# The order of a group's last step in a frequency mix: the two last pairs of S and the last spreading ahead of the fourth turn

## The chip, the cores and the metric

The kernel runs on one core of one Trainium2 chip. The metric is the device time of one execution in microseconds (us). Lower is better.

## What is computed

The input is x of 16 batches x 16 channels x 256 x 256 in float32. Two layers follow each other, each adding something to its group-normalised input. Only the first one matters here:

```python
alpha = fft2(gn(x))                                      # b i o x: batch, channel, row and column frequency
A  = 1 / (omega1 - weights_pole1)                        # o i k p
Bm = 1 / (omega2 - weights_pole2)                        # x i k q
S  = einsum('ikpq,oikp,xikq->oxik', weights_residue, A, Bm)
output_residue1 = einsum('biox,oxik->bkox', alpha, S)    # the mix: 16x16 matrix for every frequency (o, x)
x1 = ifft2(output_residue1).real
...                                                      # x2, a second term from the poles
x  = x + x1 + x2 / Nx / Ny
```

The second layer (two convolutions, an involution, a gate) uses most of the remaining time and is not touched.

## The kernel before, in words

The program has four parts, one after the other: `layer0_forward` (normalisation, forward transforms, tables), `layer0_mix`, `layer0_back` (inverse transform along the rows, the pole term, and the sum), and `layer1`. The change lies in `layer0_mix`.

The mix works on 33 groups of row frequencies (g = 0 to 32). A group has four row frequencies, f = 0 to 3; the last group has only one that counts. In a group these things are done:

- `poles` (L625 to L635): VectorE makes `lt`, the row factors of S, with six products (L629).
- `residues` (L639 to L653): TensorE multiplies `lt` with the table `tt` (matmuls of L643) into a PSUM buffer `ps`, for one channel k at a time; a call makes two channels. VectorE copies the odd channels into the tile `s` (L651), ScalarE the even ones (L653). Eight calls fill S for all 16 channels.
- `spread` (L617 to L620): the loaded spectrum `alc` is multiplied with a mask and written into `alb`, the right operand of the mix. There are 16 such `expand`s for a group: six on ScalarE (L605), ten on VectorE (L607). They are dealt out over the steps by a table; for f = 3 only one is left, on VectorE.
- `mix` (L655 to L672): for each of 64 x 4 column frequencies one matmul of `s` with `alb` (L665) into PSUM buffers `pg`, eight buffers' worth in sequence. ScalarE copies each into `y` (L672).
- `turn` (L674 to L688): for one f, eight TensorE transposes of `y` (L681) into two PSUM buffers `pt`. VectorE copies the first into `yt` (L687), ScalarE the second (L685).
- `columns` (L690 to L723): for one f, TensorE's inverse transform along the columns (L700) into `ph`. ScalarE copies the odd part (L709), VectorE adds and subtracts (L712, L713), and the result `h` leaves for `hd` by DMAs from POOL's queue (L720).

The groups are pipelined by hand. `s` and `lt` have one buffer, and so has `y`. S and `alb` of the next group are made during the four steps of this group, and the columns of f = 3 are put off into the mix of the next group, as a generator `between`, of which one part is taken at each of x0 = 24 and x0 = 48. `ps` of S and `pg` of the mix share four PSUM buffers, and `pt` has two.

The order of the instructions on TensorE, ScalarE, VectorE and POOL is the order in which the program calls them (`manual_schedule`); each engine works on its own list in order and waits at semaphores for the others. So the loop at L747 sets the order:

```python
for f in range(4 if more else 1):
    yt = turn(y, f)
    if more:
        if f == 3:
            spread(spectrum, f)
        for k0 in range(2 if f == 0 else 4 * f, 4 * f + 4, 2):
            residues(lt, s, k0)
        if f < 3:
            spread(spectrum, f)
        ...
    between = columns(g, f, yt)
```

In this order the step f = 3 has, on TensorE, 8 transposes and then 32 matmul records of S; on VectorE the `yt` copy, one `expand`, and the copies of channels 13 and 15; on ScalarE the `yt` copy and the copies of channels 12 and 14. After that the next group's `poles` and `mix` follow.

Of the kernel before, what the change touches and what calls it, by code (L numbers as in the profile page):

```python
# [553 lines left out]
def layer0_mix(ctx, tc, d, al, hd, tabs):  # L554
# [10 lines left out]
    def load_poles(g):  # L565
        av = ap.tile([P, 32, 4, 3], F32, tag="av", name="av")
        nc.sync.dma_start(out=av.rearrange("p k f l -> p (k f l)"), in_=avd[g])
        return av
# [21 lines left out]
    def load_spectrum(g, q):  # L590

        t = gp.tile([P, 4, 2, P], F32, tag="alc", name="alc", bufs=4)
        src = al[g].rearrange("v (j h c) b x -> h (v j) c (b x)", h=2, c=8)
        for h in range(2):
            nc.sync.dma_start(
                out=t[64 * h : 64 * h + 64].rearrange("p b e x -> p (b e x)"),
                in_=src[h, :, :, 4 * q * N : 4 * q * N + 4 * N],
            )
        return t

    def expand(t, q, j, eng):

        dst = alb.rearrange("p (x e) j b -> p b e x j", e=2)[:, 4 * q : 4 * q + 4, :, :, j]
        if eng is nc.scalar:
            eng.activation(dst, t, AF.Copy, scale=m4[:, j : j + 1])  # L605
        else:
            eng.tensor_scalar(dst, t, m4[:, j : j + 1], None, ALU.mult)  # L607
# [9 lines left out]
    def spread(spectrum, f):  # L617
        for eng, parts in zip((nc.scalar, nc.vector), spreads[f]):
            for q, j in parts:
                expand(spectrum[q], q, j, eng)  # L620

    def poles(av):


        lt = lp.tile([P, 2, C, 3, 4, 8], F32, tag="lt", name="lt")  # L625
        shape = [P, C, 4, 8]
        for h in range(2):
            for plane in range(3):
                nc.vector.tensor_tensor(  # L629
                    lt[:, h, :, plane],  # L630
                    av[:, 16 * h : 16 * h + 16, :, plane].unsqueeze(3).to_broadcast(shape),
                    m8.unsqueeze(1).unsqueeze(2).to_broadcast(shape),
                    ALU.mult,
                )
        return lt  # L635

    def residues(lt, s, k0):

        for k in range(k0, k0 + 2):  # L639
            ps = psg.tile([P, 2, N], F32, tag="pg", name="ps")  # L640
            for v in range(2):
                for h in range(2):
                    nc.tensor.matmul(  # L643
                        ps[64 * h : 64 * h + 64, v],
                        lhsT=lt[:, h, k, 1 - v : 3 - v].rearrange("p l f c -> p (l f c)"),
                        rhs=tt[:, h, k],
                        start=True,
                        stop=True,
                    )
            if k % 2:  # L650
                nc.vector.tensor_copy(s[:, :, :, k], ps.rearrange("p v x -> p x v"))  # L651
            else:
                nc.scalar.copy(s[:, :, :, k], ps.rearrange("p v x -> p x v"))  # L653

    def mix(s, y, between):  # L655


        for x0 in range(0, 64, 8):
            if x0 in (24, 48):
                next(between, None)  # L660
            ps = psg.tile([P, 8, 64], F32, tag="pg", name="pg")
            for x in range(8):
                for q in range(4):
                    i = 4 * (x0 + x) + q
                    nc.tensor.matmul(  # L665
                        ps[32 * q : 32 * q + 32, x],
                        lhsT=s[:, i].rearrange("p v k -> p (v k)"),
                        rhs=alb[:, i].rearrange("p j b -> p (j b)"),
                        start=True,
                        stop=True,  # L670
                    )
            nc.scalar.copy(y[:, :, x0 : x0 + 8], ps.rearrange("p x j -> p j x"))  # L672

    def turn(y, f):  # L674

        yt = hp.tile([P, 8, 8, C], F32, tag="yt", name="yt", bufs=2)
        for t0 in range(0, 8, 4):
            pt = pst.tile([P, 4, P], F32, tag="pt", name="pt")
            for t in range(4):
                j = 16 * f + 2 * (t0 + t)  # L680
                nc.tensor.transpose(pt[:, t], y[:, j : j + 2].rearrange("p q x -> p (q x)"), ident)  # L681
            dst = yt[:, :, t0 : t0 + 4].rearrange("p c t k -> p t c k")
            src = pt.rearrange("p t (c k) -> p t c k", k=C)
            if t0:
                nc.scalar.copy(dst, src)  # L685
            else:
                nc.vector.tensor_copy(dst, src)  # L687
        return yt  # L688

    def columns(g, f, yt):  # L690

        ph = [psh.tile([P, 2, N], F32, tag="ph", name="ph") for q in range(2)]
        for e in range(2):
            if e:
                yield
            for n, (c, v) in enumerate(((0, 0), (0, 1), (1, 0), (1, 1))):
                i = 2 * (2 * c + e) + v
                for q in range(2):
                    lanes = slice(64 * q, 64 * q + 64)
                    nc.tensor.matmul(  # L700
                        ph[q][:, e],
                        lhsT=yt[lanes, i].rearrange("p t k -> p (t k)"),
                        rhs=ix[lanes, i],
                        start=n == 0,
                        stop=n == 3,
                    )
        for q in range(2):
            odd = hp.tile([P, 2, P], F32, tag="odd", name="odd", bufs=2)
            nc.scalar.copy(odd, ph[q][:, 1].rearrange("p (v x) -> p v x", v=2))  # L709
            o = hp.tile([P, 2, 2, P], F32, tag="h", name="h", bufs=5)  # L710
            even = ph[q][:, 0].rearrange("p (v x) -> p v x", v=2)
            nc.vector.tensor_tensor(o[:, :, 0], even, odd, ALU.add)  # L712
            nc.vector.tensor_tensor(o[:, :, 1], even, odd, ALU.subtract)  # L713
            o = o.rearrange("p v h x -> p v (h x)")
            fy = 4 * g + f
            for v in range(2):

                if fy % P or v == 0:
                    part = fy // P if fy % P == 0 else v
                    nc.gpsimd.dma_start(  # L720
                        out=hd[fy % 2, part, fy % P // 2, q:nb:2].rearrange("b k x -> b (k x)"),
                        in_=o[:, v],
                    )  # L723

    E = mybir.EngineType
    with tc.manual_schedule(engines={E.PE, E.Activation, E.DVE, E.Pool}):
        spectrum = [load_spectrum(0, q) for q in range(4)]
        lt = poles(av)
        av = load_poles(1)
        s = gp.tile([P, N, 2, C], F32, tag="s", name="s")  # L730
        for k0 in range(0, C, 2):
            residues(lt, s, k0)
        for q in range(4):
            spread(spectrum, q)
        for q in range(4):
            spectrum[q] = load_spectrum(1, q)
        between = iter(())
        for g in range(NF):
            more = g + 1 < NF
            y = gp.tile([P, 64, 64], F32, tag="y", name="y")  # L740
            if more:
                lt = poles(av)
            mix(s, y, between)
            if more:
                s = gp.tile([P, N, 2, C], F32, tag="s", name="s")
                residues(lt, s, 0)
            for f in range(4 if more else 1):  # L747
                yt = turn(y, f)
                if more:
                    if f == 3:  # L750
                        spread(spectrum, f)
                    for k0 in range(2 if f == 0 else 4 * f, 4 * f + 4, 2):
                        residues(lt, s, k0)
                    if f < 3:
                        spread(spectrum, f)
                    if g + 2 < NF:
                        if f == 0:
                            av = load_poles(g + 2)
                        spectrum[f] = load_spectrum(g + 2, f)
                between = columns(g, f, yt)  # L760
                if f < 3:
                    for _ in between:
                        pass
# [774 lines left out]
```

## Time and profile before

| | us |
|---|---|
| three timed runs, median (lowest to highest) | 7067.28 (7063.57 to 7080.53) |
| the profiled execution: its own time | 7081.88 |
| its span | 7080.1 |
| mix: first L665 matmul to last | 1414.4 to 2906.8 |
| one group, from mix to mix | 43.7 to 52.2 |

In the profile PE is TensorE's matmul part, PEld its weight loads, DVE is VectorE, ACT is ScalarE, POOL is GpSimd and SP the queue from which most loads are started. A row of a timeline has the start in us from the beginning of the span, the length, the engine, the line, the operation, the tiles written and read, the number of instructions merged into the row, and in brackets the idle time ahead of it with the engine and line that ended it ("issue" means that the engine waited for nothing that the profile shows). A matmul in float32 leaves two records, so a count of x32 is 16 matmuls. What is done once in a group counts 32 or 33 times in the whole.

### The profile page before, as it was taken

The numbers are of one execution on the slowest core, as the hardware profiler recorded it, in microseconds if no ns is written. First come the engines' busy times: TensorE is split into PE (matmuls) and PEld (weight loads), VectorE is DVE, ScalarE is ACT, GpSimd is POOL, SyncE is SP. The second block draws the span as 40 slices with busy tenths as digits, with TensorE's granted clock in tenths as the row PEclk, the third lists the DMA queues.
The fourth block names the chain that finished last, engine by engine and source line by source line (L and its number), as shares of the span: only waits on it lengthen the run. The fifth ranks groups of instructions, "written<-read, shape, count | busy, mean of one in ns | idle before, by whom it ended". The sixth has DMA issues, their size and how long they took to land. (4 is left out here: it accounts for less than half of the span.)

```text
span 7080.1 us, 144599 instructions
## 1 busy us (share of the span) xinstructions
PE 6544.7 (92%) x55592; PEld 3663.3 (52%) x55592; DVE 5608.9 (79%) x10346; ACT 3835.5 (54%) x5996; POOL 3521.3 (50%) x4614
## 2 busy tenths in 40 slices
PE   7889999899999998899979999999999999999996
PEld 5777778666667666677733333333333333333331
DVE  8999985466667666688878888888888888888885
ACT  2223333365666665322266666666666676666671
POOL 2334445412222222466655666667666667665663
PEclk9899999999999999999989999999999999999998
DMA  3344444433333333699968888889888889888886
GB/s 99 112 115 123 125 120 123 132 95 92 100 99 102 98 96 92 207 326 326 326 191 248 260 257 269 277 278 282 268 257 265 277 281 278 277 258 264 277 272 212
DMA packets 716083, 1443.41 MB, mean 204 GB/s; under 512 B 98954, under 2 KB 525254, under 8 KB 673638
## 3 DMA queue, kind: packets, MB, share of 16 engines
q1 hardware_dynamic: 567206, 959.76, 44.3%
q0 software_dynamic: 148192, 474.40, 21.3%
q8 instruction: 444, 7.27, 0.4%
q14 instruction: 241, 1.97, 0.1%
HBM read 877.12 MB, written 556.47 MB: 202 GB/s over the span
## 5 line engine op out<-in xcount | busy, mean ns | idle before, releaser
L1085 ACT ACTIVATE wide<-c,b 32x512 f32<-32x512 f32 x2176 | 1477.6, 679 | 314.0 <-PE c L1037 265.2
L1116 DVE TENSOR_TENSOR top<-pd,t 32x512 f32<-32x512 f32 x2176 | 1504.0, 691 | 55.8 <-DMA cf<-top 3.2
L1037 PE MATMUL c<-z,w 102*128 102x512 f32 x2048 | 996.4, 618 | 110.5 <-ACT wide L1085 89.0
L1113 DVE TENSOR_TENSOR t<-pd,r 64x512 f32<-64x512 f32 x1088 | 743.8, 684 | 349.0 <-PE pd L1105 322.8
L1097 POOL COPY wide<-wide 32x1031 f32<-32x1031 f32 (+1 forms) x576 | 581.2, 1009 | 882.6 <-ACT wide L1085 855.5
L1105 PE MATMUL pd<-wide,dw 128*128 128x512 f32 x2048 | 994.4, 607 | 13.0 <-DVE top L1116 12.0
L720 POOL DMA_DIRECT2D hd<-h x512 | 323.5, 639 | 1207.1 <-DVE h L713 1182.6
L1037 PEld LDWEIGHTS c<-z,w 102*128 102x128 f32 x2048 | 370.6, 191 | 695.2 <-issue 457.9
L1185 PE MATMUL c2ps<-rows,c 128*32 128x512 f32 x6144 | 721.9, 602 | 5.6 <-DVE odd L1212 5.6
L1105 PEld LDWEIGHTS pd<-wide,dw 128*128 128x128 f32 x2048 | 382.8, 193 | 576.5 <-issue 417.2
L1056 ACT ACTIVATE bot<-c,b 128x512 f32<-128x512 f32 x544 | 343.9, 683 | 462.2 <-issue 383.3
L1098 POOL COPY wide<-wide 32x1031 f32<-32x1031 f32 (+1 forms) x576 | 574.0, 997 | 33.5
L700 PE MATMUL ph<-ix,yt 64*128 64x256 f32 x4128 | 506.6, 393 | 6.1 <-issue 5.4
L643 PE MATMUL ps<-tt,lt 128*64 128x256 f32 x4224 | 495.4, 385 | 13.3 <-DMA tt<-td 10.4
L313 PE MATMUL px<-wxn,u 128*64 128x256 f32 x4224 | 482.9, 380 | 8.1 <-ACT o L320 8.1
L207 PE MATMUL pu<-fy,eo 128*128 128x128 f32 x2048 | 427.0, 292 | 26.4 <-DVE u L224 21.8
L700 PEld LDWEIGHTS ph<-ix,yt 64*128 64x128 f32 x4128 | 395.9, 191 | 93.7 <-issue 46.1
L1185 PEld LDWEIGHTS c2ps<-rows,c 128*32 128x32 f32 x6144 | 175.4, 109 | 513.3 <-issue 407.8
L873 POOL TENSOR_TENSOR x<-x,o 128x512 f32<-128x512 f32 x256 | 323.7, 1265 | 217.4 <-DVE o L872 199.3
L607 DVE TENSOR_SCALAR alb<-alc,m 128x1024 f32<-128x1024 f32 x330 | 420.0, 1397 | 0.0
L214 PE MATMUL pv<-at,eo 128*128 128x128 f32 x2048 | 413.9, 285 | 0.0
L651 DVE COPY s<-ps 128x512 f32<-128x512 f32 x264 | 265.4, 1023 | 186.9 <-PE ps L643 169.7
(220 smaller groups left out, 11732.0 us busy)
## 6 DMA issues: line engine op xcount, KB each, us to landing
rows<-cf SPq DMA_DIRECT2D x128, 2176.0 KB
z<-zn SPq DMA_DIRECT2D x768, 257.8 KB
cf<-top POOLq DMA_DIRECT2D x512, 240.0 KB, 6.8
cf<-bot POOLq DMA_DIRECT2D x96, 840.0 KB, 11.0
alc<-al SPq DMA_DIRECT2D x264, 256.0 KB
zn<-zb SPq DMA_DIRECT2D x128, 516.0 KB
o<-zn SPq DMA_DIRECT2D x128, 516.0 KB
z<-in_x SPq DMA_DIRECT2D x64, 1024.0 KB
```

What stands on the lines that cost most here:

```text
L207: nc.tensor.matmul(pu[:, xh, e].rearrange("p v m -> p (v m)"), lhsT=lhs, rhs=fy[:, e], start=True, stop=True,)
L313: nc.tensor.matmul(ps[64 * k : 64 * k + 64, :, h], lhsT=u[:, h, part, g0 + j + k].rearrange("p f c -> p (f c)"), rhs=wxn[:, h, part], star ...
L643: nc.tensor.matmul(ps[64 * h : 64 * h + 64, v], lhsT=lt[:, h, k, 1 - v : 3 - v].rearrange("p l f c -> p (l f c)"), rhs=tt[:, h, k], start= ...
L700: nc.tensor.matmul(ph[q][:, e], lhsT=yt[lanes, i].rearrange("p t k -> p (t k)"), rhs=ix[lanes, i], start=n == 0, stop=n == 3,)
L1037: nc.tensor.matmul(ps[:, a], lhsT=w, rhs=z[:k, c : c + 2, 0:N], start=True, stop=True)
L1085: nc.scalar.activation(self.feat[64 - 32 * q : 96 - 32 * q, f, self.groups[g], :H], ps[q][32 * f : 32 * f + 32], AF.Mish, bias=b1[0][32 * ...
L1097: nc.gpsimd.tensor_copy(flat[0:32, f, 1:m], flat[64:96, f, 0 : m - 1])
L1098: nc.gpsimd.tensor_copy(flat[96:128, f, 0 : m - 1], flat[32:64, f, 1:m])
L1105: nc.tensor.matmul(ps, lhsT=dwt if self.tail else dw, rhs=self.feat[:, f, cs, :H], start=True, stop=True,)
L1113: nc.vector.tensor_tensor(t[64:128], ps[:64], self.r[:, cs], ALU.mult)
L1116: nc.vector.tensor_tensor(self.top[32 * f : 32 * f + 32, cs, q], ps[lanes], t[lanes], ALU.add)
L1185: nc.tensor.matmul(ps[32 * j : 32 * j + 32], lhsT=w[:, blk], rhs=src[:, 4 * j + blk : 4 * j + blk + 4, x : x + H], start=(i, blk) == (0, 0 ...
```

## The change

In the step f = 3 of every group but the last, the one `expand` and the two `residues` calls (channels 12 to 15) are called ahead of `turn(y, 3)`, and no longer after it. The other steps keep their order. In the step's own order:

- TensorE: 32 matmul records of S, then 8 transposes (before: 8, then 32).
- VectorE: `expand` (L607), copies of channels 13 and 15 (L651), then `yt` (L687). Before: `yt`, then `expand`, then the copies.
- ScalarE: copies of channels 12 and 14 (L653), then `yt` (L685). Before: `yt`, then the copies.
- SP and POOL: the same order of DMAs as before.

Number and kind of instructions stay as they are. Two waits change their place: the mix's first matmul waits for S as before, and the first L700 matmul of the put-off columns, at x0 = 24, waits for `yt` by itself; before, the wait for S covered it.

```diff
             for f in range(4 if more else 1):
+                if more and f == 3:
+                    spread(spectrum, f)
+                    for k0 in (12, 14):
+                        residues(lt, s, k0)
                 yt = turn(y, f)
                 if more:
-                    if f == 3:
-                        spread(spectrum, f)
-                    for k0 in range(2 if f == 0 else 4 * f, 4 * f + 4, 2):
+                    for k0 in range(2 if f == 0 else 4 * f, 4 * f + 4, 2) if f < 3 else ():
                         residues(lt, s, k0)
                     if f < 3:
                         spread(spectrum, f)
```

## The prediction, made before the changed kernel was run

> **What bounds the kernel now.** I read the page's slices first, then the waits of the stretch that the change touches, then the timelines of one group on VectorE, TensorE and ScalarE. The slices are 177 us each. The mix has the lines L607 to L720 and fills slices 9 to 17, from 1414 us (first matmul of L665) to about 2910 us.
>
> ```profile
> PE   7889999899999998899979999999999999999996
> DVE  8999985466667666688878888888888888888885
> ```
>
> TensorE is 80 to 90% busy there and VectorE 60 to 80%, so neither is simply full. The page's chain of waits does not help: the pieces that it lists start after 3565 us, behind the mix. So I ask who waits for whom between 1420 and 2880 us, for TensorE alone (total us, times, longest):
>
> ```profile
> PE pg L665 <- issue: 73.6, 40, 4.6
> PE pg L665 <- DVE s L651: 44.3, 31, 1.5
> ```
>
> The second row is the one that the change aims at: once in every group, TensorE stands 44.3 / 31 = 1.43 us in front of the first L665 matmul of the mix, until VectorE has copied the last column of S. The first row is a stop within the mix for which no engine is named; I come back to it. Here is VectorE around the mix that starts at 2157.35 us (start, length, instruction, idle time before it):
>
> ```profile
> 2147.68 1.03 DVE L651 COPY s<-ps 128x512 f32<-128x512 f32 x1 [0.71 <-PE ps L643]
> 2148.56 3.77 DVE L607 TENSOR_SCALAR alb<-alc,m 128x1024 f32<-128x1024 f32 x3
> 2152.14 0.44 DVE L712 TENSOR_TENSOR h<-ph,odd 128x256 f32<-128x256 f32 x1
> ...
> 2153.16 0.40 DVE L713 TENSOR_TENSOR h<-ph,odd 128x256 f32<-128x256 f32 x1
> 2153.50 0.67 DVE L687 COPY yt<-pt 128x512 f32<-128x512 f32 x1
> 2154.09 1.43 DVE L607 TENSOR_SCALAR alb<-alc,m 128x1024 f32<-128x1024 f32 x1
> 2155.35 1.86 DVE L651 COPY s<-ps 128x512 f32<-128x512 f32 x2
> 2157.07 3.66 DVE L629 TENSOR_TENSOR lt<-av,m 128x512 f32<-128x512 f32 x6
> ```
>
> From 2147.68 to 2160.73 us VectorE has no idle time. The two S copies (channels 13 and 15) end at 2157.21 and the mix starts 0.14 us later. In front of them stands the copy of the fourth turn, yt at 2153.50, which the mix does not need. TensorE in the same time:
>
> ```profile
> 2147.56 3.72 PE L700 MATMUL ph<-ix,yt 64*128 64x256 f32 x32
> 2151.22 1.09 PE L681 MATMUL pt<-ident,y 128*128 128x128 f32 x8
> 2152.24 3.67 PE L643 MATMUL ps<-tt,lt 128*64 128x256 f32 x32
> 2157.35 2.89 PE L665 MATMUL pg<-alb,s 128*32 128x64 f32 x192 [1.44 <-DVE s L651]
> 2160.17 2.00 PE L700 MATMUL ph<-ix,yt 64*128 64x256 f32 x16
> ```
>
> It is done with S at 2155.91. So at this spot VectorE is the bound and TensorE has 1.44 us to spare. I looked at this stretch in all 32 groups: yt starts 3.84 to 3.89 us ahead of the mix and alb 3.24 to 3.30, the last S copy ends 0.15 ahead of it. The pattern does not vary.
>
> [...] 12 of the 32 groups hold a half-speed stretch of 2.9 to 6.8 us.
>
> **The change part by part.** Nothing is added or taken away. [...]
>
> 1. *VectorE.* The yt copy moves behind alb and the two S copies. It costs its 0.67 us, but overlaps its neighbours: alb starts 0.59 to 0.60 us after it (2153.50 to 2154.09). alb needs only spectrum data loaded long before, so it starts where yt did. Each S copy must also find its matmuls done. TensorE now starts S at about 2151.3 instead of 2152.24 and ends channel 13 by about 2153.2, channel 15 by about 2155.0; VectorE would reach them at 2154.75 and 2155.6. Both are there. The last S copy ends at 2157.21 - 0.60 = 2156.61: **0.60 us** gained at the release.
>
> 2. *TensorE.* S (3.67 us) first, then the eight transposes (1.09 us): the same 4.7 us, ending at about 2156.0, before VectorE's release. The PSUM buffers that S takes were read by the S copies of channels 8 to 11, the last of which ended at 2148.71, so S meets no new wait. The mix can start at about 2156.75, not 2157.35. TensorE's idle time falls from 1.44 to about 0.75 us, and this leftover is VectorE's still.
>
> 3. *ScalarE.* Its half of the turn goes behind S copies 12 and 14:
>
> ```profile
> 2151.36 0.68 ACT L709 COPY odd<-ph 128x256 f32<-128x256 f32 x2
> 2152.34 0.58 ACT L685 COPY yt<-pt 128x512 f32<-128x512 f32 x1 [0.31 <-PE pt L681]
> 2153.37 1.04 ACT L653 COPY s<-ps 128x512 f32<-128x512 f32 x1 [0.44 <-PE ps L643]
> 2155.10 1.02 ACT L653 COPY s<-ps 128x512 f32<-128x512 f32 x1 [0.68 <-PE ps L643]
> 2158.51 0.59 ACT L672 COPY y<-pg 128x512 f32<-128x512 f32 x1 [2.39 <-PE pg L665]
> ```
>
> The S copies can run about 0.9 us earlier, yt follows the transposes at about 2156.2 and ends by 2156.8; the first y copy comes at about 2157.9. I cost this at nothing; the cover is the 2.39 us in which ScalarE was idle.
>
> 4. *A wait that is new.* The columns of f = 3 inside the mix (L700 at 2160.17) so far had yt for certain once S was there; now their first matmul waits for both yt copies itself. VectorE's ends at about 2156.5 + 0.7 = 2157.2, the columns would come at 2160.17 - 0.60 = 2159.57. Slack 2.3 us: nothing. Behind it on TensorE the rest of the mix would stand, so a delay would cost in full.
>
> 5. *What comes after yt on VectorE.* The poles' six products (lt) start and end as before, at 2160.73, as the sum ahead of them is the same; S of the next group needs lt at 2171.24 - 0.60. Nothing. SP's next spectrum load follows alb and can only come earlier.
>
> Sum: 32 groups x 0.60 = **19.2 us less**. The profiled execution took 7081.9 us (span 7080.1), 14.6 above the median of the three timed runs, 7067.3. Against its own time the sum gives 7062.7; carried over to the median, **7048**. The stages around the mix are not touched and start from its end.
>
> **What is not shown directly: the instruction supply.** Within the mix a matmul pair takes about 15 ns, so 128 pairs, one block, are used up in 1.9 us. The group before shows what follows:
>
> ```profile
> 2109.00 2.06 PE L665 MATMUL pg<-alb,s 128*32 128x64 f32 x131 [1.42 <-DVE s L651]
> 2113.58 1.90 PE L665 MATMUL pg<-alb,s 128*32 128x64 f32 x61 [2.52 <-issue]
> ```
>
> The stops stand at multiples of 256 instructions; in the mix the packets of q8 follow each other at 3.4 to 3.7 us, and matmuls go on about 1.4 us after one has landed (in this group a packet starts at 2111.25, lands at 2112.25, and work goes on at 2113.58). In most groups the first packet starts 1.9 to 2.6 us after the first mix matmul, with or without other stops: it is asked for as the mix starts, so it moves with it. Bounds: none of the 0.60 is lost, or all of it in a group where the fetch is asked for earlier. Those (packets 3 to 8 us ahead of the mix) land before they are needed. I take a loss of zero and keep the whole 19.2 us for the range.
>
> **Rivals.**
> *A larger supply loss.* If the fetch keeps its own time, the earlier mix merely waits longer at the first stop. For it: the stops are larger than the wait removed. Against it: the packets' constant distance from the mix start. Time: 7067 if all is lost, 7058 if half.
> *Slower: more half-speed windows.* Groups with a half-speed stretch last 48.7 us on average, the other 20 last 44.8, so one costs up to 3.9 us (some of that is the supply stop at another place). A shorter group shifts the mix against the windows. Five more such groups eat the gain; 12 more, which makes 24 of 32, give 12 x 3.9 - 19.2 = +28: 7095. Against it: all but the first of these stretches begin 4.6 to 7.3 us after a mix start, behind the supply stop, not behind the wait that shrinks. They can become fewer just as well.
> *The whole wait goes.* If VectorE ran S with more overlap than now, TensorE could gain up to 1.44 us: 32 x 1.44 = 46, so 7021. Against it: alb and both S copies stay ahead of the mix.
>
> **How the numbers follow.** 0.3% is 21.2 us, about what a measurement of this kernel can tell from no change; the sum lies just inside. The forecast has 0.72, the supply loss 0.15, more half-speed windows 0.08, the larger gain 0.05. Two windowed groups more or less in a run (8 us) can push the forecast over the bound: of its 0.72 I give 0.27 to faster and 0.44 to the same. With the others: faster 0.32, same 0.63, slower 0.05. The range runs from 7034 (the forecast with nearly four windowed groups fewer) to 7068 (all lost).
>
> **What would show it.** In the waits, L665 on S falls from 1.43 to about 0.8 us each; on VectorE alb follows L713 and yt follows S; the count of half-speed groups stays near 12. I am wrong if L665's wait keeps its length, if L700 in the mix waits for yt, or if the issue row grows by about 19 us.

## The result, and the profile after

The changed kernel takes 7063.18 us (median of 20 runs, 7053.91 to 7075.37), the kernel before 7076.52 us in the same comparison (20 runs, 7063.57 to 7082.51). The ratio is 0.9983, 95% interval 0.9976 to 0.9990. It is faster, by 12 us from the ratio (7 to 17) and by 13.3 us from the medians, where the forecast's sum was 19.2.

The profiled execution took 7066.55 us, its span 7064.8. The slices of the page look as before:

```profile
PE   7889999899999999899979999999999999999996
DVE  8999985466666666688878888888888888888885
```

The waits of TensorE in the stretch of the mix (1420 to 2870 us; total us, times, longest) show what the change did and what it did not do:

```profile
PE pg L665 <- issue: 74.3, 40, 4.8
PE pg L665 <- DVE s L651: 26.4, 31, 0.9
```

The wait for S has fallen from 44.3 to 26.4 us, 0.85 us each time in place of 1.43. The stop without a named engine looks as large as ever, 74.3 against 73.6 us, but this row has only the stops that end with an L665. The put-off columns (L700) run inside the mix too, and their stops have grown; before (1420 to 2880 us) and after:

```profile
PE ph L700 <- issue: 5.4, 4, 3.2
```

```profile
PE ph L700 <- issue: 9.9, 7, 2.9
```

Both rows together have gone from 79.0 to 84.2 us. VectorE's timeline around the mix that starts at 2144.95 us:

```profile
2135.87 1.03 DVE L651 COPY s<-ps 128x512 f32<-128x512 f32 x1 [0.70 <-PE ps L643]
2136.75 3.77 DVE L607 TENSOR_SCALAR alb<-alc,m 128x1024 f32<-128x1024 f32 x3
2140.30 0.47 DVE L712 TENSOR_TENSOR h<-ph,odd 128x256 f32<-128x256 f32 x1
...
2141.31 0.45 DVE L713 TENSOR_TENSOR h<-ph,odd 128x256 f32<-128x256 f32 x1
2141.64 1.49 DVE L607 TENSOR_SCALAR alb<-alc,m 128x1024 f32<-128x1024 f32 x1
2142.92 1.89 DVE L651 COPY s<-ps 128x512 f32<-128x512 f32 x2
2144.66 0.66 DVE L687 COPY yt<-pt 128x512 f32<-128x512 f32 x1
```

The expand (L607) now starts right behind the last h product, the two S copies follow, and yt comes last. TensorE there:

```profile
2135.75 3.73 PE L700 MATMUL ph<-ix,yt 64*128 64x256 f32 x32
2139.40 3.67 PE L643 MATMUL ps<-tt,lt 128*64 128x256 f32 x32
2143.01 1.09 PE L681 MATMUL pt<-ident,y 128*128 128x128 f32 x8
2144.95 2.89 PE L665 MATMUL pg<-alb,s 128*32 128x64 f32 x192 [0.85 <-DVE s L651]
2147.77 2.00 PE L700 MATMUL ph<-ix,yt 64*128 64x256 f32 x16
```

S comes first, the transposes second, and the mix starts 0.85 us after them.

To see where the gain goes I split each group into three parts by the records of the trace and took the mean of 32 groups; the last two rows lie within the mix:

| part of a group, us | before | after |
|---|---|---|
| copy of channel 11 (L651) to first L665 of the mix | 9.66 | 9.08 |
| the mix, first to last L665 | 14.82 | 15.08 |
| last L665 to the next copy of channel 11 | 21.75 | 21.67 |
| idle time of TensorE within the mix | 2.48 | 2.65 |
| time at half clock within a group's mix | 1.69 | 1.66 |

Half clock stands for the stretches in which the trace's clock record has TensorE at 0.5 of full speed; in the profile of before an L665 record takes 314 ns in them and 219 ns outside (medians), and the records start 26.6 and 14.2 ns apart on average, gaps over 100 ns left out.

The first part has no scatter: 9.64 to 9.69 before, 9.07 to 9.10 after. This is the 0.58 us that the change releases, 32 x 0.58 = 18.6 us. The third part is 21.61 us in most groups of both. The mix itself scatters, and it got longer by 0.26 us, of which 0.17 are idle time: this is where the missing part is.

### The profile page after: what moved, and what is told of

The parts are those of the page before. It is cut to its first block, busy times and chain, and to the rows that moved or that the text cites. A ratio compares the mean times of both kernels' runs of the same rounds, so it can differ in the third digit from the quotient of the medians.

```text
span 7064.8 us, 144662 instructions
## 1 busy us (share of the span) xinstructions
PE 6544.4 (93%) x55592; PEld 3663.8 (52%) x55592; DVE 5610.5 (79%) x10346; ACT 3836.7 (54%) x5996; POOL 3516.5 (50%) x4614
## 3 DMA queue, kind: packets, MB, share of 16 engines
q1 hardware_dynamic: 567206, 959.76, 44.3%
q14 instruction: 241, 1.97, 0.1%
## 5 line engine op out<-in xcount | busy, mean ns | idle before, releaser
L700 PE MATMUL ph<-ix,yt 64*128 64x256 f32 x4128 | 509.6, 393 | 10.7 <-issue 9.9
L643 PE MATMUL ps<-tt,lt 128*64 128x256 f32 x4224 | 493.2, 384 | 10.4 <-DMA tt<-td 9.2
L700 PEld LDWEIGHTS ph<-ix,yt 64*128 64x128 f32 x4128 | 397.0, 191 | 99.3 <-issue 51.3
L607 DVE TENSOR_SCALAR alb<-alc,m 128x1024 f32<-128x1024 f32 x330 | 419.6, 1395 | 0.0
L651 DVE COPY s<-ps 128x512 f32<-128x512 f32 x264 | 266.3, 1027 | 183.3 <-PE ps L643 166.3
```

The lines of the kernel that those rows point to most:

```text
L643: nc.tensor.matmul(ps[64 * h : 64 * h + 64, v], lhsT=lt[:, h, k, 1 - v : 3 - v].rearrange("p l f c -> p (l f c)"), rhs=tt[:, h, k], start= ...
L700: nc.tensor.matmul(ph[q][:, e], lhsT=yt[lanes, i].rearrange("p t k -> p (t k)"), rhs=ix[lanes, i], start=n == 0, stop=n == 3,)
```

## The experiments

**VectorE's part alone (e3).** TensorE and ScalarE keep the transposes first; VectorE's copy of the fourth turn is held back:

```diff
-                yt = turn(y, f)
+                later = [] if more and f == 3 else None
+                yt = turn(y, f, later)          # the VectorE copy is put into later
 ...
                         residues(lt, s, k0)
+                    for dst, src in later or ():
+                        nc.vector.tensor_copy(dst, src)
```

> Of the change only VectorE's part: there the yt copy of f = 3 goes behind the spread and the two S copies; TensorE and ScalarE keep transposes first. If TensorE's part is needed too: the last S copy cannot start before its matmuls end (2155.91 us plus about 0.15 in the profile of before), so the wait of L665 falls by only 0.1 to 0.2 us and the time by 3 to 6 us. If VectorE's list alone decides: 0.58 us less per group, and 12 to 19 us less in all, as with the whole change.

Measured: 7066.6 us against 7071.03, ratio 0.9992 (0.9984 to 1.0000). The group's first part is 9.44 us: 0.22 gained of 0.58. VectorE and then TensorE in one group:

```profile
2149.14 0.98 DVE L651 COPY s<-ps 128x512 f32<-128x512 f32 x1
2150.36 1.01 DVE L651 COPY s<-ps 128x512 f32<-128x512 f32 x1 [0.24 <-PE ps L643]
```

```profile
2151.52 2.89 PE L665 MATMUL pg<-alb,s 128*32 128x64 f32 x192 [1.20 <-DVE s L651]
```

VectorE was early, but waited 0.24 us for TensorE's S, which stood behind the transposes. So TensorE's half of the change is needed for the larger part of the 0.58 us, as the prediction's first step had it. It is this wait that shows it: in time e3 cannot be told from e4, the next run. TensorE's half without VectorE's was not run.

**The spread alone (e4).**

```diff
+                if more and f == 3:
+                    spread(spectrum, f)
                 yt = turn(y, f)
                 if more:
-                    if f == 3:
-                        spread(spectrum, f)
```

> Of the change only the spread of f = 3 ahead of the fourth yt copy on VectorE; both stay ahead of the S copies. All theories: the S copies end when they did, the wait of L665 stays at 1.43 us, the time within 4 us of the kernel before. If it moves by more, something other than the release of the mix is at work.

Measured: 7066.63 us against 7071.03, ratio 0.9996 (0.9988 to 1.0005): no difference. The wait stays at 1.42 us:

```profile
PE pg L665 <- DVE s L651: 44.1, 31, 1.4
```

This run gives a second profile of the old release time, and that is worth more than its ratio: its mix is 14.36 us, with 20 us at half clock summed over the 32 groups, where the profile of before has 14.82 and 54. So the half clock differs between executions (20 against 54 us here), and a mix length from one profile is uncertain by some 0.2 us, an estimate: half of what these two lie apart.

**The changed kernel once more (e9).**

> The changed kernel itself once more, for a second profile of it. All theories: 0.9983 of the kernel before, within 0.0015. In the profile the wait of L665 on S is 0.85 us. If the mixes of its first profile were long by chance (53 us of half-speed time, as in the kernel before), half-speed time and mix length here differ from it as much as the two profiles of the old release time do (before: 54 us of half-speed time and a mix of 14.8 us; e4: 20 us and 14.4 us); theory S expects the mix above 14.4 us in any case.

Measured on another chip: 7059.92 us against 7073.37, ratio 0.9983 (0.9976 to 0.9991), the same as before. Mix 14.83 us, 41 us at half clock. The three profiles with the old transposes-first order on TensorE (before, e3, e4) have mixes of 14.82, 14.60 and 14.36 us, the two of the new order 15.08 and 14.83. The mean differs by 0.36 us, in the direction that the timing asks for: 18.6 less 12 leaves 6.6 us to explain, or 0.2 per group. Most of this is idle time: within a mix TensorE stands still for 2.48, 2.44 and 2.40 us in the three old profiles and for 2.65 and 2.55 in the two new ones, 0.16 us more on average, or 5 us over 32 groups. A part of half clock is not clear of noise: on this chip the granted clock over a whole execution is 0.9772 on average in 19 runs of the kernel before and 0.9769 in 15 of the changed kernel, which is 2 us of lost clock (0.0003 of 7066 us) with a standard error of 1.4.

**The loads out of the mix (e1, e2).** The spectrum loads of q = 2 and 3 and the poles' load, which are issued by SP as soon as their buffers are free and then run beside the first part of the mix, go to ScalarE's queue behind the last y copy (the poles in f = 0):

```diff
             mix(s, y, between)
+            if more and g:
+                for q in (2, 3):
+                    spectrum[q] = load_spectrum(g + 1, q, nc.scalar)
 ...
-                            av = load_poles(g + 2)
-                        spectrum[f] = load_spectrum(g + 2, f)
+                            av = load_poles(g + 2, nc.scalar)
+                        if f < 2:
+                            spectrum[f] = load_spectrum(g + 2, f)
```

e1 does this to the new order, e2 to the old one.

> The new order, with the spectrum loads of q = 2 and 3 and the load of the poles issued from ScalarE's queue behind the last y copy of the mix (q = 2, 3) and in the step f = 0 (poles), so that these loads no longer run beside the first 6 us of the mix. Theory A (the loads run beside the instruction packets of the mix, and the new order moves the mix 0.58 us further into them): the mix itself, first to last L665, gets shorter than the 15.08 us of the new order on average, by 0.3 us or more (10 us or more in all), and as short as in the old order with late loads. Theory B (the shortfall against 19 us is chance of the half-speed windows): the mix keeps about 15 us in undisturbed groups of equal place in the instruction blocks, the time stays within 4 us of the new order's. Against the kernel before: A 0.9960 or less, B about 0.9980.

> The old order with the same late loads as e1. Theory A: faster than the kernel before by 5 to 30 us through a shorter mix, and e1 is faster than this one by the whole of what VectorE's release gains, 32 x 0.58 = 18.6 us. Theory B: within 4 us of the kernel before; e1 is faster by about 12 us, as new and old were.

Measured: e2 7034.6 us (ratio 0.9945, 0.9932 to 0.9957), e1 7015.03 us (0.9919, 0.9906 to 0.9933). Both are much faster than the kernel before (7071.03 here), and e1 is 19.6 us faster than e2: 7012.0 to 7020.9 against 7029.2 to 7038.8, four and five runs. Without the loads beside the mix, the same change of order gives the whole 18.6 us as far as so few runs can tell: the scatter leaves some 5 us either way, and in the two profiles the stage, from the first L665 to the last, is 16.5 us shorter, with a mix that is 0.14 us longer. Theory A had the difference right, but not the size: the 36 us of e2 lie above its 5 to 30. Its reading of how the gain arises is only half right, as the profiles show. Here the place of a mix in TensorE's instruction stream counts. The page of before has this row for queue q8 (packets, MB, share):

```profile
q8 instruction: 444, 7.27, 0.4%
```

That is 16,384 bytes a packet, and the trace has 113,680 TensorE records (matmuls, weight loads and its sequencer's), 256 to a packet. Counted from the trace's first TensorE instruction in blocks of 256, the 37 stops of over 0.8 us that end with an L665 within the mixes of before all end at 0.75 or 0.76 of a block. Take one mix at nearly the same place in these blocks, 0.55 to 0.62 of one. TensorE in the kernel before, and the busy times of the mix's first 6 us there (us, PE, PEld, DVE, ACT, POOL, granted clock, DMA share, GB/s):

```profile
2247.38 2.43 PE L665 MATMUL pg<-alb,s 128*32 128x64 f32 x156 [1.44 <-DVE s L651]
2251.76 0.75 PE L665 MATMUL pg<-alb,s 128*32 128x64 f32 x36 [1.95 <-issue]
```

```profile
2247.40:2253.40 6.00, 4.05 (x200) 3.72 (x202) 3.35 (x6) 1.75 (x3) 0.00 (x0) 1.00 0.53 149
```

The old order with late loads:

```profile
2211.80 2.43 PE L665 MATMUL pg<-alb,s 128*32 128x64 f32 x156 [1.44 <-DVE s L651]
2215.34 0.75 PE L665 MATMUL pg<-alb,s 128*32 128x64 f32 x36 [1.11 <-issue]
```

```profile
2211.80:2217.80 6.00, 4.88 (x208) 4.32 (x208) 3.37 (x6) 1.76 (x3) 0.00 (x0) 1.00 0.07 23
```

The DMA engines fall from 53 to 7% busy, and the stop from 1.95 to 1.11 us. The same for the changed kernel and for the new order with late loads:

```profile
2236.81 2.28 PE L665 MATMUL pg<-alb,s 128*32 128x64 f32 x147 [0.86 <-DVE s L651]
2241.06 0.87 PE L665 MATMUL pg<-alb,s 128*32 128x64 f32 x45 [1.97 <-issue]
```

```profile
2236.80:2242.80 6.00, 4.02 (x200) 3.75 (x202) 3.98 (x7) 1.75 (x3) 0.00 (x0) 1.00 0.57 173
```

```profile
2205.43 2.28 PE L665 MATMUL pg<-alb,s 128*32 128x64 f32 x147 [0.84 <-DVE s L651]
2209.04 0.87 PE L665 MATMUL pg<-alb,s 128*32 128x64 f32 x45 [1.33 <-issue]
```

```profile
2205.40:2211.40 6.00, 4.64 (x206) 4.31 (x208) 4.00 (x7) 1.76 (x3) 0.00 (x0) 1.00 0.15 45
```

Here it falls from 1.97 to 1.33 us. For all groups whose mix starts between 0.27 and 0.79 of a block, nearly half of them, the trace gives these medians after the first mix matmul:

| us after the mix start | first instruction packet starts | first stop ends |
|---|---|---|
| before, e3, e4 (old order on TensorE) | 2.20, 2.15, 2.07 | 4.70, 4.48, 4.40 |
| after, e9 (new order) | 2.32, 2.46 | 4.88, 4.89 |
| e2 (old order, late loads) | 1.20 | 3.78 |
| e1 (new order, late loads) | 1.51 | 3.82 |

So with the loads beside the mix the packet starts about 1 us later (2.07 to 2.20 us behind the mix start against 1.20 in the old order, 2.32 and 2.46 against 1.51 in the new one), and in the new order it starts 0.25 to 0.31 us later behind the mix start than in the old one, with the loads as without. Some groups fare worse: in groups 1 to 31 the first packet starts more than 3.2 us after the mix start 6, 7 and 7 times in the three old profiles and 8 times in each of the new ones, and never in e1 and e2 (at most 2.60 us). The shorter stops go along with a second effect, on the clock. The stage from 1460 to 2820 us in before, after, e1 and e2:

```profile
1460.00:2820.00 1360.00, 1242.60 (x23727) 945.01 (x23715) 903.86 (x1285) 832.35 (x997) 294.17 (x467) 0.98 0.33 97
```

```profile
1460.00:2820.00 1360.00, 1256.92 (x23753) 953.68 (x23742) 917.07 (x1299) 845.54 (x1009) 297.57 (x472) 0.98 0.34 98
```

```profile
1460.00:2820.00 1360.00, 1281.85 (x24477) 973.59 (x24467) 954.05 (x1350) 872.17 (x1046) 310.13 (x492) 1.00 0.35 102
```

```profile
1460.00:2820.00 1360.00, 1267.25 (x24281) 962.24 (x24271) 941.84 (x1336) 859.53 (x1034) 306.77 (x487) 1.00 0.34 101
```

In e1 and e2 TensorE has its full clock (1.00): beyond the first group, no mix holds a half-clock stretch, where before had 11 such groups and the changed kernel 11. Groups without half clock differ less between the kernels (13.43 us of mix before, 13.96 after, 13.30 in e2, 13.44 in e1), but leaving the others out also leaves out the longest stops. Over all 32 groups the mix of e2 is 1.53 us shorter than before, of which 0.90 are idle time and 0.63 faster matmuls; from the changed kernel to e1 it is 1.65 us, 0.99 and 0.66. So the shorter stops are the larger part, the clock the smaller.

What comes ahead of a half-clock stretch can be read from the traces. In each of the twelve profiles all stretches begin on a grid of 3.413 us, to within 0.07 us over the whole execution. I took every window of this grid at full clock from the second mix to the last, in all twelve. TensorE was busy for less than 0.40 of the window 35 times, and each time half clock followed; between 0.40 and 0.55 it followed 22 times of 101; above 0.55, in 5738 windows, never. So in these traces half clock followed stops of which enough fell into one window; a stop of 1.5 us, by itself, leaves the window 0.56 busy, an estimate from (3.413 - 1.5) / 3.413. How the grid lies against the stops differs between executions: the last grid point ahead of the first L665 is 0.46 us before it in the profile of before, 1.58 us in that of the changed kernel.

**The place in the block held fixed (e5 to e8).** With small matmuls and one or two repeated transposes a group is filled up to 7 blocks of 256 instructions, so that all mixes start at the same place; the filling costs about 27 us a group in both orders, where 1 to 3 were expected. The loads are late, as in e1 and e2.

```diff
                 for h in range(2):
+                    for _ in range(fill(n, k, 2 * v + h)):     # 46 in a group, spread over k = 0 to 11
+                        nc.tensor.matmul(ps[64 * h : 64 * h + 32, v, :64],
+                            lhsT=lt[:, h, k, 1 - v : 3 - v].rearrange("p l f c -> p (l f c)")[:, :32],
+                            rhs=tt[:, h, k, :64], start=True, stop=True)
                     nc.tensor.matmul(
```

> Old order, late loads as in e2, and 46 or so small matmuls (128x64 into a part of ps that the real matmul overwrites) and one or two repeated transposes added to a group, so that a group has 1792 TensorE instructions on average, 7 blocks of 256: every mix starts at the same place in a block, 0.63 of one (counted from the program's first recorded TensorE instruction). In the late-load kernels the first stop in the mix at this place ends about 3.5 us after the mix start in the old order and 3.7 to 3.8 in the new one, and the first packet starts at 1.1 or 1.45. This run is the base for e6; the added matmuls cost 1 to 3 us per group in both.

> New order with the same additions, mixes at 0.63 of a block. Theory S (at such places the packet that the mix waits for is asked for before the mix starts, at a time that the change does not move): the stop ends 0.3 to 0.45 us later after the mix start than in e5, and this kernel is faster than e5 by only 4 to 9 us. Rival (the packet is asked for by the start of the mix and moves with it, as the prediction had it): the mix keeps its length, faster than e5 by 18.6 us = 32 x 0.58.

> As e5 with every mix at 0.91 of a block, where the first packet lands before the mix starts and the first stop comes only about 8.2 us into it. Mix 12.5 us against about 14.5 in e5: 50 to 70 us faster than e5. Base for e8.

> As e6 at 0.91 of a block. Both theories: the packets that the mix waits for here are asked for within the mix and move with it, the mix keeps its length to 0.1 us, and the whole 32 x 0.58 = 18.6 us shows against e7 (16 to 20). If the gain is as small as in e6, the place in the block is not what takes it.

Measured: e5 7939.07 us, e6 7930.71: the new order gains 8.4 us at 0.63 of a block (4 and 5 runs, whose ranges overlap; their profiles' stages differ by 7.0). e7 7876.62, e8 7856.85: it gains 19.8 us at 0.91 (ranges apart). One mix of e5 and one of e6, with L677 for L665:

```profile
2649.57 2.23 PE L677 MATMUL pg<-alb,s 128*32 128x64 f32 x145 [1.42 <-DVE s L663]
2653.25 0.87 PE L677 MATMUL pg<-alb,s 128*32 128x64 f32 x47 [1.46 <-issue]
```

```profile
2642.53 2.23 PE L677 MATMUL pg<-alb,s 128*32 128x64 f32 x145 [0.83 <-DVE s L663]
2646.68 0.87 PE L677 MATMUL pg<-alb,s 128*32 128x64 f32 x47 [1.92 <-issue]
```

VectorE's wait is shorter by 0.59 us and the stop longer by 0.46. Over 31 groups the first packet starts 1.16 us after the mix start in e5 and 1.52 in e6, and the first stop ends at 3.69 and 3.93 on average. So 0.25 of the 0.59 us goes to the first stop at such places, a little less than Theory S had (0.3 to 0.45). The mixes of e6 were 0.42 us longer in all, of which 0.13 are idle time and 0.29 slower matmuls; 7 of them held a half-clock stretch and one in e5, and those without differ by 0.08 us only. The runs' granted clock agrees: 0.9815 on average in the four of e5, 0.9802 in the five of e6. So here most of the loss came as half clock, which Theory S did not name. In e7 and e8 a packet starts 4 to 6 us ahead of the mix, so the first stop comes later, for instance in e7:

```profile
2693.70 2.89 PE L677 MATMUL pg<-alb,s 128*32 128x64 f32 x192 [1.39 <-DVE s L663]
2696.52 2.00 PE L713 MATMUL ph<-ix,yt 64*128 64x256 f32 x16
2698.45 2.43 PE L677 MATMUL pg<-alb,s 128*32 128x64 f32 x157
2702.30 0.75 PE L677 MATMUL pg<-alb,s 128*32 128x64 f32 x35 [1.42 <-issue]
```

Its packet starts 2.31 us after the mix start in e7 and 2.32 in e8, so it moved with the mix. Mix 13.18 us in e7, 13.04 in e8: nothing is lost. The gains fit Theory S and not the rival, which the prediction had taken; that 8.4 us fell within the 4 to 9 of Theory S is in part luck, with most of the loss from half clock and ranges that overlap. Between e5 and e7 the mixes differ by 1.8 us, 58 us in all, about as expected.

**One more step (e10).** e1, with the last expand moved out of f = 3:

```diff
-        (((1, 1), (2, 0)), ((1, 2), (1, 3), (2, 1))),
+        (((1, 1), (2, 0)), ((1, 2), (1, 3), (2, 1), (3, 3))),
         (((3, 0), (3, 1)), ((2, 2), (2, 3), (3, 2))),
-        ((), ((3, 3),)),
+        ((), ()),
```

> e1 with one more step out of VectorE's way: the expand (3, 3) goes from the step f = 3 to f = 1, so that only the h products stand between the last spread and the two S copies. VectorE's release could come up to 1.27 us earlier; TensorE's own S and transposes end 0.85 us ahead of the mix in e1, so up to 0.7 us are left to gain, 22 us in all. Theory S: at about half the places in a block a part goes to the stop again, 12 to 20 us faster than e1, 6995 to 7003. If VectorE cannot make up the added 1.27 us in f = 1 (it waits 0.7 us for TensorE in each of f = 1 and 2): less than 5 us.

Measured: 7007.66 us, ratio 0.9908 (0.9893 to 0.9924); 7.4 us faster than e1 by the medians, on another chip, which neither 12 to 20 us nor less than 5 had right. The wait for S is nearly gone, but the stop has grown from e1's 45.0 us:

```profile
PE pg L665 <- issue: 52.9, 36, 2.8
PE pg L665 <- DVE s L651: 6.4, 31, 0.2
```

```profile
2205.44 2.28 PE L665 MATMUL pg<-alb,s 128*32 128x64 f32 x147 [0.21 <-DVE s L651]
2209.47 0.87 PE L665 MATMUL pg<-alb,s 128*32 128x64 f32 x45 [1.75 <-issue]
```

The group's first part is 8.24 us, 0.84 less than in e1, 27 us in all. The mix is 13.96 us, 0.53 more, and the rest of the group is 0.20 longer. The first packet, at the places between 0.27 and 0.79, starts 2.13 us after the mix start (1.51 in e1), the stop ends at 4.41 (3.82), and 5 of the 14 groups there hold half-clock stretches again, where e1 had none. So here too a mix that starts earlier gives part of the gain back in a longer mix. It is still the fastest kernel of this study, 0.9% below the kernel before.

## Why the prediction was right or wrong

- **The release (steps 1 to 3): right.** Predicted 0.60 us, measured 0.58; the wait of L665 predicted at about 0.75 to 0.8 us, measured 0.85. Here the prediction's own sum gives 0.84: TensorE's work keeps its length, so 1.44 less 0.60 is left. The order on VectorE and the free time on ScalarE are as described. e3 shows that VectorE's half alone gives only 0.22 us.
- **The new wait for yt (step 4) and the poles (step 5): right.** L700 waits for no yt in the mix and L643 for no lt: neither row appears among TensorE's waits from 1420 to 2870 us.
- **The instruction supply: wrong, and this is the step that failed.** "I take a loss of zero", because the first packet stood 1.9 to 2.6 us behind the mix start in most groups, so "it is asked for as the mix starts, so it moves with it". It did not: of the 0.58 us by which the mix moved the packet followed 0.33 with the loads in place (2.14 us behind the mix start in the three old profiles, 2.39 in the two new ones), 0.27 with late loads, and 0.23 in e6 against e5. The first stop then ended 0.36, 0.04 and 0.24 us later behind the mix start. And 0.94 us (old order) and 0.88 us (new order) of the distance went when the loads were moved. That part of what calls for the packet lies ahead of the mix, where the change moves nothing, fits this but is not shown. With the loads in place the whole change loses 6.6 us of its 18.6 to a longer mix (2 to 12, from the ratio's interval), about 5 of them as idle time. The supply rival, which named this with half the gain lost, was nearer than the forecast.
- **Half-clock windows.** The rival that their number rises is not borne out with the loads in place: 54, 38 and 20 us in the old order, 53 and 41 in the new, and a granted clock over the runs of one chip that differs by 2 us of lost clock, with a standard error of 1.4. In the old order the mixes get shorter with them (14.82, 14.60 and 14.36 us). But the prediction treated them as a throw of dice beside the stops. The windows of the grid tie them to the stops, and so do e1, e2 and e10: at the places of the table no such group while the stops end by 3.8 us, 5 when they end at 4.4.
- **The anchor: the larger part of the miss in numbers.** 7048 was set off from a median of three runs, 7067.3; twenty runs have 7076.5. Of the 15.2 us between forecast and measurement, 9.2 come from this and 6.0 from the sum. Against the profiled execution's own time the sum gave 7062.7, within 0.5 us of the measurement, but by luck: that execution, at 7081.9, stood at the top of the range of those twenty, 5.4 us above their median, and this hides the loss.

What stays open: which of the loads (spectrum or poles) does the harm, since they were moved together; whether it is their time or their queue, ScalarE's in place of SP's, since both changed at once; what calls for an instruction packet; and what decides about half clock after windows that are 0.40 to 0.55 busy.

## What to carry to other kernels

When a wait ahead of a dense burst of small matmuls gets shorter, look at what feeds the burst apart from its operands: here the instruction packets, which started about 1 us later while data loads ran beside them (2.07 to 2.20 us behind the mix start against 1.20). A constant distance between two events is no proof that one causes the other; ask what else comes at that time, and move that. And before a small change is priced against its baseline, see how far single runs of the baseline lie apart.

## What the runs showed of the hardware that was not expected

- With the data loads beside the mix its first instruction packet started about 1 us later (2.07 to 2.20 us behind the mix start against 1.20 in the old order), and moving 1.2 MB of loads per group to behind the mix made the kernel 36 us (old order) or about 45 us (new order) faster without any change in computation.
- TensorE fell to half clock in the middle of a stage in which it is over 90% busy (1242.60 of 1360 us in before). Each time it had been busy for no more than 0.53 of the 3.413 us window before; under 0.40 half clock always followed (35 of 35 windows), above 0.55 never (0 of 5738).
- 46 extra matmuls of 128x64 in a group cost about 27 us, 0.58 us each, where the mix has 96 of this form in 2.89 us, 0.03 us each. In the timeline of e5 one of them and the larger matmul behind it take 0.81 us (2666.47 to 2667.28), where the larger one alone took 0.23 in before (16 in 3.67 us). Each writes 32 partitions of `ps` just ahead of the larger matmul, which writes over them; whether this is the reason was not tested.
